# Fifteen block products for eighteen in layer 1, and its context in quarters of the array

## The chip, the cores and the metric

The kernel runs on one core of a Trainium2 chip. The metric is the device time of one execution in microseconds; the time before is the median of 3 runs. The engines are named as in the profile: PE multiplies matrices, PEld loads its weights, DVE, ACT and POOL work on vectors, and SP issues the DMAs. Products are in fp32 throughout.

## The reference

The program is two graph layers on 128 graphs of 64 nodes with 768 features. After each layer comes a residual and a layer norm. Cut to what is computed:

```python
def layer0(x, adj):                       # 12 heads of 64
    h = einsum('bnd,ade->bane', x, W)
    th = tanh(h)
    a = th @ w_src + swap(th @ w_dst)
    a = where(a >= 0, a, 0.2 * a)
    a = softmax(where(adj, a, -999.0))
    f = elu(concat_heads(a @ h + b))
    gate = sigmoid(x @ H_w.T + H_b)
    return gate * f + (1 - gate) * x

def layer1(x, adj):                       # 6 heads of 128
    q, k, v = heads(x @ Wq + bq), heads(x @ Wk + bk), heads(x @ Wv + bv)
    s = q @ k.T / sqrt(128) + where(adj, 0, -9e15)
    return concat_heads(softmax(s) @ v) @ Wf + bf

x = layernorm(x + layer0(x, adj))
x = layernorm(x + layer1(x, adj))
```

Layer 0 has two dense products of 768x768 (W and H_w), layer 1 four (Wq, Wk, Wv, Wf). The attention products are small: 64 nodes by 64 nodes for each head.

## The kernel before

**Tiles.** Two graphs fill the 128 partitions of a token tile, so there are 64 tiles, two tiles make a pair (32 pairs), and in phase B two pairs make a group (16 groups).

**Dense products.** Every 768x768 product of a pair is done by a 2x2x2 scheme: the two tiles are the rows, the two halves of the inner dimension and the two halves of the outputs (384) the other axes, and seven block products stand for eight. `Product` takes them one at a time (`matmuls(i)`, `evict(i)`), each as three matmuls of 128 rows (`CH` = 3). The sums of token blocks that the scheme needs are four additions on POOL (`token_sums`: S0 to S3, 384 columns each). The sums of weight blocks are made once for each weight (`weight_sums`: four additions of 1152 columns). Partial results leave PSUM by ACT copies ("snap") and DVE additions. PSUM tiles are called X (two buffers), Y and Z (one each), and pa or pb for the small products.

**Phase A** does layer 0, and layer 1's V product at its end, because its weights fit beside the others. It spills to DRAM: the normalized x (`x1_d`), its transposed form (`xT_d`), the four sums S (`S_d`) and v (`v_d`). Layer 0's aggregate (L476) multiplies 64x64 blocks: its row half and its column half pick a quarter of the array, 24 matmuls for a tile. The input is cut into chunks for the transposes (`chunk0`, L308) by features that lie 6 apart.

**Phase B** does the rest of layer 1. For a group it loads T (`T4`, one buffer) and S, then runs the Q and K products for three column blocks j of each half: weights stand still and 256 token columns (two pairs) move. `scores` then takes 8 matmuls for each head (L749), six batches a group. `sm_top` and `sm_total` do the softmax: maximum and subtraction on DVE, exp on ACT, sum and reciprocal on DVE, scaling on POOL (L771). `probs` transposes the probabilities (L776) and writes them by four ACT copies into `pt1`, a tile that holds a block diagonal of two graphs with zeros beside it, so that `context` can use whole 128x128 matmuls (L794), six for a tile. The output product F of a pair then adds into the residual tile x, to which POOL has added the bias before (`add_bf`, L674). `layernorm` takes its statistics on DVE and three small instructions on POOL (L221, L223, L224), `normalize` is one ACT instruction (L228), and SP stores the tile.

**Order.** Nothing is scheduled by a planner. Each phase is a table of events: `at(step, f)` puts a function into a step, and `run` calls the steps in order. The functions emit instructions on all engines, so the table fixes the order of each engine's queue; semaphores do the rest. Phase B has 35 steps a group before:

```python
for j in range(3):
    at(o + 7 * j, lambda d=d, j=j: start_qk(d, j))
    for i in range(7):
        at(o + 7 * j + i, lambda d=d, i=i: dense_qk(d, i))
    at(o + 7 * j + 7, lambda d=d, j=j: scores(d, j, 0))
    at(o + 7 * j + 8, lambda d=d, j=j: scores(d, j, 1))
```

The output products of a group begin 56 and 63 steps after its first step, which are steps 21 to 34 of the next group, beside that group's last scores and its softmax; the last group draws them forward. The weights Wq and Wk come in at the end of phase A (`load_early`), in the places of layer 0's weights, and POOL makes their sums 30 and 46 steps after the last pair's first step.

## Time and profile before

| | |
|---|---|
| median of 3 runs | 3132.32 us (3130.44 to 3134.71) |
| the profiled execution's own time | 3132.67 us |
| its span, first to last instruction | 3130.7 us |
| instructions in the profile | 42352 |
| first Q matmul of phase B | 1603.84 us |
| PE busy | 3039.9 us, 97% of the span |
| POOL busy | 1292.9 us: 938.67 before 1603.8 us, 354.28 after |
| DVE busy | 1557.3 us: 999.82 before 1603.8 us, 557.45 after |
| ACT busy | 962.9 us |
| DMA | 309.40 MB, mean 99 GB/s |

Times are in microseconds unless marked ns. A row of the groups has line, engine, operation, output and inputs by the program's names, shapes and count, then busy time, the mean ns of one, and the idle time of the engine before these with what ended it. A row of the timeline has its start, its length, the engine, the line and what is merged in it. A row of the waits has who waited for whom, the total, the number of times and the longest. Matmuls are pipelined and overlap in the records, so the mean ns of one is longer than the distance between two starts. The digits are tenths of busy time in 40 slices of 78 us.

### The profile page before, as it was taken

What the parts mean: (1) busy time and instruction counts of PE and PEld (TensorE: products, weight loads), DVE (VectorE), ACT (ScalarE), POOL (GpSimd) and SP (SyncE); (2) the same over time, 40 slices, a digit from 0 to 9 for tenths busy, and PEclk for the clock granted to TensorE, in tenths of its full rate; (3) what the DMA queues carried; (4) which work ended last, traced back from release to release, by engine and by line L of the source; (5) the groups of instructions that cost most, each with busy time, mean ns of one, the idle gap of its engine ahead of it and who ended that gap; (6) DMA issues with size and microseconds to landing.
All of it is one profiled execution on the core that took longest, in us unless ns stands there. A gap on an engine that the chain in (4) does not pass through costs nothing.

```text
span 3130.7 us, 42352 instructions
## 1 busy us (share of the span) xinstructions
PE 3039.9 (97%) x16164; PEld 2124.8 (68%) x16164; DVE 1557.3 (50%) x2717; ACT 962.9 (31%) x1901; POOL 1292.9 (41%) x1207
## 2 busy tenths in 40 slices
PE   7999999999999999999878999999999999999998
PEld 4566666666666666666557777887777887777885
DVE  4666666666666666666612333334333334333334
ACT  2344444444344444443312221222221222221122
POOL 4656556566566566565532122222122222122223
PEclk9999999999999999999889999999999999999999
DMA  4233233333233333333432222212222212222211
GB/s 152 87 112 123 89 115 117 99 115 117 94 115 117 100 115 106 106 120 99 147 139 82 87 76 92 91 62 102 87 75 94 91 61 102 87 73 95 91 62 61
DMA packets 186218, 309.40 MB, mean 99 GB/s; under 512 B 89504, under 2 KB 115104, under 8 KB 186016
## 3 DMA queue, kind: packets, MB, share of 16 engines
q1 hardware_dynamic: 186016, 306.69, 29.2%
q8 instruction: 128, 2.10, 0.3%
q14 instruction: 74, 0.61, 0.1%
HBM read 167.81 MB, written 126.22 MB: 94 GB/s over the span
## 4 chain that ended last, share of the span: by engine, by line
PE 89%; DVE 4%; DMA 1%; ACT 1%; POOL 1%; issue 0%; SPq 0%; POOLq 0%; DVEq 0%
PE X L147 45%; PE Y L147 24%; PE Z L147 9%; PE pb L794 3%; PE pa L308 3%; PE pb L749 2%; PE pa L476 2%; PE pa L458 1%; DVE st L216 1%; PE pb L776 1%; DVE snap L820 1%; DVE s L762 1%; DVE sm L768 0%; DVE mx L761 0%; ACT s L763 0%
## 5 line engine op out<-in xcount | busy, mean ns | idle before, releaser
L147 PE MATMUL X<-w,S 128*128 128x384 f32 x1728 | 614.2, 492 | 6.0 <-DVE v L356 3.7
L147 PEld LDWEIGHTS X<-w,S 128*128 128x128 f32 x1728 | 320.5, 191 | 241.8 <-DVE gt L337 19.9
L147 PE MATMUL X<-S,w 128*128 128x256 f32 x1728 | 396.5, 379 | 0.0
L147 PEld LDWEIGHTS X<-S,w 128*128 128x128 f32 x1728 | 326.0, 190 | 43.1
L221 POOL TENSOR_TENSOR rstd<-rstd,neg_half 128x1 f32<-128x1 f32 x128 | 70.5, 551 | 652.7 <-DVE rstd L220 652.7
L771 POOL TENSOR_TENSOR s<-s,rs 128x768 f32<-128x768 f32 x32 | 47.1, 1473 | 627.3 <-DVE rs L770 584.6
L228 ACT ACTIVATE x<-x,shift,rstd 128x768 f32<-128x768 f32 x128 | 131.3, 1026 | 295.8 <-POOL shift L224 295.8
L147 PE MATMUL X<-w,T 128*128 128x384 f32 x576 | 209.0, 500 | 8.5 <-ACT T L309 7.3
L147 PE MATMUL X<-w,Sc 128*128 128x384 f32 x576 | 204.7, 492 | 12.0 <-DVE snap L820 12.0
L147 PE MATMUL Z<-w,T 128*128 128x384 f32 x576 | 205.3, 493 | 0.0
L147 PE MATMUL Y<-w,S 128*128 128x384 f32 x576 | 204.8, 492 | 0.0
L147 PE MATMUL Y<-T,w 128*128 128x256 f32 x864 | 202.2, 379 | 0.0
L147 PE MATMUL Y<-w,T 128*128 128x384 f32 x576 | 201.5, 486 | 0.0
L690 ACT COPY snapq<-X 128x256 f32<-128x256 f32 x192 | 71.5, 372 | 363.4 <-PE X L147 363.1
L147 PEld LDWEIGHTS Y<-T,w 128*128 128x128 f32 x864 | 163.0, 190 | 21.5
L147 PEld LDWEIGHTS X<-w,Sc 128*128 128x128 f32 x576 | 105.7, 190 | 86.7 <-DVE snap L820 21.9
L147 PEld LDWEIGHTS Y<-w,T 128*128 128x128 f32 x576 | 109.4, 190 | 76.3
L720 DVE SCALAR_TENSOR_TENSOR q<-X,bq_c,snapq 128x256 f32<-128x256 f32 x48 | 23.2, 484 | 267.8 <-PE X L147 267.8
L147 PEld LDWEIGHTS X<-w,T 128*128 128x128 f32 x576 | 107.5, 196 | 70.8 <-ACT T L309 9.0
L447 POOL TENSOR_TENSOR s<-s,rs 128x768 f32<-128x768 f32 x64 | 94.8, 1481 | 146.6 <-DVE rs L446 146.6
L147 PE MATMUL X<-T,w 128*128 128x256 f32 x576 | 138.2, 390 | 13.6 <-DMA T<-xT_d 13.6
L147 PEld LDWEIGHTS Y<-w,S 128*128 128x128 f32 x576 | 105.4, 191 | 62.2
(132 smaller groups left out, 5431.1 us busy)
## 6 DMA issues: line engine op xcount, KB each, us to landing
x<-in_x_dram SPq DMA_DIRECT2D x64, 384.0 KB
s<-dst_d SPq DMA_DIRECT2D x128, 192.0 KB
x_d<-x SPq DMA_DIRECT2D x64, 384.0 KB
xT_d<-T SPq DMA_DIRECT2D x64, 384.0 KB
S_d<-S SPq DMA_DIRECT2D x32, 768.0 KB
v_d<-v SPq DMA_DIRECT2D x128, 192.0 KB
T<-xT_d SPq DMA_DIRECT2D x32, 768.0 KB
S<-S_d SPq DMA_DIRECT2D x32, 768.0 KB
```

The lines of the kernel that those rows point to most:

```text
L147: nc.tensor.matmul(o, self.lhsT(i, c), rhs, start=first and c == 0, stop=last and c == CH - 1, skip_group_check=True,)
L216: nc.vector.bn_stats(st[:, half, :], r[:, halves(half)])
L221: nc.gpsimd.tensor_tensor(rstd, rstd, neg_half, ALU.pow)
L228: nc.scalar.activation(r, r, AF.Identity, bias=shift, scale=rstd)
L308: nc.tensor.transpose(ps[:, c, :], chunk(src, k), ident)
L447: nc.gpsimd.tensor_tensor(self.s, self.s, self.rs[:, :, None].to_broadcast([P, A, S]), ALU.mult)
L458: nc.tensor.transpose(ps[:, jj, :], self.s[:, 2 * j : 2 * j + 2, :].rearrange("p h m -> p (h m)"), ident,)
L476: nc.tensor.matmul(self.pos[h2][own, j, :], self.pt[rws, j, own], rhs, start=True, stop=True,)
L690: nc.scalar.copy(t, ps)
L749: nc.tensor.matmul(pc[own, q, i, :], qT[:, i, q, own], kT[:, i, q, own], start=True, stop=True)
L771: nc.gpsimd.tensor_tensor(s, s, rs[:, :, None].to_broadcast([P, A, S]), ALU.mult)
L794: nc.tensor.matmul(pc[:, jj, :], v[:, hd * P : (hd + 1) * P], pt1[:, hd, :], start=True, stop=True)
```

## The change

Phase B's three dense products (Q, K and the output product) use a 2x3x3 scheme: two tiles, three blocks of 256 inner features, three blocks of 256 outputs, and fifteen block products where eighteen would be plain. The tables `SUMS`, `WEIGHT_SUMS` and `STEPS` hold the scheme. A block product is two matmuls of 128 rows and 256 columns. Four PSUM chains accumulate and are read between steps: each step names the chain, and the outputs to which the chain's present value is added or from which it is subtracted. For Q and K the first touch of an output is an ACT instruction and the others are DVE additions; for the output product all 16 are DVE additions into the residual tile.

The eleven token sums are now made on POOL in phase B, for each group (512 columns, `group_sum`) and for each pair of the output product (256 columns, `pair_sum`); in the first group DVE makes seven of them. S is no longer stored and loaded. The weights of phase B have fourteen sums of 512 columns each (`weight15_sum`) in place of four. `S{k}`, `Sc{k}`, `T4` and the two tiles of scores have one buffer each.

The context works on 64x64 blocks: v is loaded so that the two heads of a couple lie in the two halves of the partitions (four DMAs a tile), the probabilities are copied once and not laid out as a block diagonal, and 24 matmuls for a tile go to the quarters of the array. Q and K now go one after the other, in two passes j over 15 steps each, and scores come twice a group, three batches in a row. A group has 90 steps; the output products of a group take steps 60 to 89 of the next one. In phase A the PSUM tiles X, Y and Z share one pool of four, and `chunk0` takes features that lie 3 apart, with W read in the same order.

```diff
+STEPS = [   # sum or block, weight slot, chain, first, last, outputs touched
+    (6, 4, 2, True, False, (0, -1, 0, 0, 0, 0)),
+    (7, 13, 3, True, False, (0, 0, 1, 0, 0, 0)),
...
-    psX = ctx.enter_context(tc.tile_pool(name="psX", bufs=2, space=bass.MemoryType.PSUM))
-    psY = ctx.enter_context(tc.tile_pool(name="psY", bufs=1, space=bass.MemoryType.PSUM))
+    psX = ctx.enter_context(tc.tile_pool(name="psX", bufs=4, space=bass.MemoryType.PSUM))
...
-            return src.rearrange("p (q c) -> p c q", c=NC)[:, k, :]
+            return src.rearrange("p (h q c) -> p h c q", h=2, c=CH)[:, k // CH, k % CH, :]
...
-                nc.sync.dma_start(S_d[d["p"]], d["S"])
...
-        at(o + 30, lambda: weight_sums(early[0], nc.gpsimd))
-        at(o + 46, lambda: weight_sums(early[1], nc.gpsimd))
+        for k in range(len(WEIGHT_SUMS)):
+            at(o + 18 + k, lambda k=k: weight15_sum(early[0], k, nc.gpsimd))
+            at(o + 32 + k, lambda k=k: weight15_sum(early[1], k, nc.gpsimd))
...
+        def group_sum(d, k, eng):
+            r0, r1, op = SUMS[k]
+            t = k1.tile([P, 2, 2, P], F32, name=f"S{k}")
+            eng.tensor_tensor(t, group_part(d, r0), group_part(d, r1), op)
+            d["S"][k] = t
+        def pair_sum(d, q, k):
+            r0, r1, op = SUMS[k]
+            t = k1.tile([P, 2, P], F32, name=f"Sc{k}")
+            nc.gpsimd.tensor_tensor(t, pair_part(d, q, r0), pair_part(d, q, r1), op)
+            d["Sc", q, k] = t
...
+            def step(self, i):
+                r, slot, chain, start, stop, coefs = STEPS[i]
+                if start:
+                    self.acc[chain] = psX.tile(self.shape, F32, name="X")
+                ps = self.acc[chain]
+                for c in range(2):
+                    nc.tensor.matmul(ps, self.lhsT(r, slot, c), self.rhs(r, slot, c),
+                                     start=start and c == 0, stop=stop and c == 1,
+                                     skip_group_check=True)
+                for j, coef in enumerate(coefs):
+                    if coef and j not in self.begun:
+                        self.first(j, coef > 0, ps)
+                        self.begun.add(j)
+                    elif coef:
+                        self.add(j, coef > 0, ps)
...
-            for half in range(2):
-                pc = psa.tile([P, CH, P], F32, name="pb")
-                for jj in range(CH):
-                    hd = half * CH + jj
-                    nc.tensor.matmul(
-                        pc[:, jj, :], v[:, hd * P : (hd + 1) * P], pt1[:, hd, :], start=True, stop=True
-                    )
+            for j in range(CH):
+                for g in range(2):
+                    own = slice(g * S, (g + 1) * S)
+                    for half in range(2):
+                        for h2 in range(2):
+                            rws = slice(h2 * S, (h2 + 1) * S)
+                            cols = slice(half * S, (half + 1) * S)
+                            nc.tensor.matmul(pcs[h2][cols, j, own], v[rws, g, j, cols],
+                                             pt[rws, j, own], start=True, stop=True)
...
+        R = len(STEPS)
+        N = 6 * R
...
+                at(o - 29, lambda g=g: load_T(g))
+                at(o - 35, lambda g=g: load_adj(g))
+            for k in range(len(SUMS)):
+                eng = nc.vector if g == 0 and k % 3 else nc.gpsimd
+                at(o - 24 + 2 * k, lambda d=d, k=k, eng=eng: group_sum(d, k, eng))
...
+                at(e + 3 + 6 * q, lambda d=d, q=q: sm_top(d, q))
+                at(e + 6 + 6 * q, lambda d=d, q=q: sm_total(d, q))
+                pr = o + (4 * R + 14 + 12 * q if last else N + 4 + 16 * q)
+                f = o + ((6 if last else 10) + q) * R
...
+                        s = max(f - R + max(SUM_STEPS[: k + 1]) + 1, pr + 13)
+                    at(s, lambda d=d, q=q, k=k: pair_sum(d, q, k))
+                at(f - (3 if last else 12), lambda g=g, q=q: load_x(g, q))
+                at(f - (1 if last else 5), lambda d=d, q=q: add_bf(d, q))
...
+                    s = f + R + 1 + 3 * i
+                    at(s, lambda d=d, q=q, i=i: norm1(d, q, i))
+                    at(s + 2, lambda d=d, q=q, i=i: norm2(d, q, i))
```

In the last lines, o is the group's first step, e is o + 62, q the pair of the group and f the step at which a pair's output product begins.

## The prediction

> **What bounds the kernel now.** I read the busy shares first, then PE's waits, then PE's timeline for the pace of each kind of matmul.

> ```profile
> PE 3039.9 (97%) x16164; PEld 2124.8 (68%) x16164; DVE 1557.3 (50%) x2717; ACT 962.9 (31%) x1901; POOL 1292.9 (41%) x1207
> ...
> PE   7999999999999999999878999999999999999998
> ...
> POOL 4656556566566566565532122222122222122223
> ```

> PE shows 9 in 35 of 40 slices. POOL falls from 4 to 6 tenths in phase A (slices 1 to 20) to some 2 in phase B: that looks like room.

> ```profile
> PE X L147 <- DMA T<-xT_d: 13.6, 1, 13.6
> PE X L147 <- DVE snap L820: 12.0, 16, 1.7
> ```

> Of phase B, these and two waits of the first group (7.9 us, on POOL's softmax scaling and ACT's pt) are all that the view lists for PE. The first is the start of phase B, the second 0.75 us in each of 16 groups. Phase B runs from the first Q matmul (1603.84 us in the timeline) to the end; T loads of neighbouring groups stand 94.0 us apart (2019.58 and 2113.56). So phase B is priced by PE's passes. An fp32 matmul is two passes, two records.

> ```profile
> 2009.03 2.75 PE L147 MATMUL X<-S,w 128*128 128x256 f32 x12
> ...
> 2011.62 2.75 PE L147 MATMUL Y<-S,w 128*128 128x256 f32 x12
> ...
> 2024.00 0.69 PE L749 MATMUL pb<-k,q 128*64 128x64 f32 x16
> ...
> 2024.62 2.20 PE L147 MATMUL Z<-w,cT 128*128 128x384 f32 x6
> ...
> 2026.75 0.69 PE L749 MATMUL pb<-k,q 128*64 128x64 f32 x16
> ```

> Starts count, since matmuls overlap: 12 passes of 256 columns take 2.59 us, **216 ns each**. Six passes of 384 columns take 1.935 us (next fence), **322.5 ns each**. From one score batch to the next, 2.75 us, less those six passes, leaves **0.81 us** for a batch of 8 score matmuls. Single records inside the batch start 7 and 52 ns apart, so its matmuls take 8 x 59 = 0.47 us and the change of array mode 0.34.

> ```profile
> 1520.52 2.10 PE L147 MATMUL Z<-w,T 128*128 128x384 f32 x6
> 1522.45 2.10 PE L147 MATMUL X<-w,S 128*128 128x384 f32 x6
> ```
> ```profile
> 1503.43 2.10 PE L147 MATMUL X<-w,T 128*128 128x384 f32 x6
> ...
> 1506.32 2.20 PE L147 MATMUL Z<-w,T 128*128 128x384 f32 x6
> 1508.36 2.10 PE L147 MATMUL X<-w,S 128*128 128x384 f32 x6
> ```
> ```profile
> 2056.23 1.50 PE L794 MATMUL pb<-pt,v 128*128 128x128 f32 x12
> 2057.57 1.46 PE L147 MATMUL Z<-T,w 128*128 128x256 f32 x6
> ```

> In the middle stretch, layer 0's aggregate of one tile lies between the products: 24 matmuls of 64x64 in the array's quarters. 1508.36 - 1503.43 less two products (3.87) leaves **1.06 us a tile**, mode changes included. Layer 1's context with full matmuls takes 2 x 0.67 = **1.34 us a tile**: 12 passes, 1.34 us from the first start to the next line's start.

> [...] 48 quarter passes in 1.06 us, and 0.34 us of mode change around a score batch. [...] at 2045.46 POOL starts a norm only as the softmax scaling ahead of it ends, though DVE had its input ready at 2045.2. [...] The softmax subtraction, of one shape, takes 958 ns in phase B (L762) and 1374 in phase A (L437), where POOL is busy[...] Layer 0's transposes at a stride of 6 floats start 136 ns apart, unit-stride ones 109.5.

> **The change, PE's work, per group (16 of them).** Q and K: 2 x 3 x 21 matmuls become 2 x 2 x 30, of 256 columns: (240 - 252) x 0.216 = -2.6 us. Output product: 42 matmuls of 384 columns become 60 of 256: 120 x 0.216 - 84 x 0.3225 = 25.9 - 27.1 = -1.2. Context: 4 tiles x (1.06 - 1.34) = -1.1. Scores: 6 batches of 8 become 2 of 24: 2 x (24 x 0.059 + 0.34) = 3.5 against 4.9, -1.4. Transposes of the probabilities stay. Sum -6.2 us, **-99 us** in all. Phase A's chunks at a stride of 3 floats instead of 6: 12 transposes x 32 pairs x at most 27 ns = 0 to -10; I take -5. One shared pool of four PSUM tiles for X, Y and Z keeps a product's distance before a tile is reused: nothing. The S tiles' stores (768 KB a pair) and loads go, v comes in 16 DMAs a group for 4, at some 0.4 us each on SP: the DMA share is 1 to 3 tenths in phase B, SP issues a few times in 94 us, and after the start PE waits for no DMA, so nothing. pt's four copies become one on ACT, which is at 1 to 2 tenths: nothing.

> **What it adds: POOL.**

> ```profile
> L674 POOL TENSOR_TENSOR x<-x,bf_bc 128x768 f32<-128x768 f32 x64 | 114.0, 1813 | 6.3 <-DMA x<-x_d 6.3
> L771 POOL TENSOR_TENSOR s<-s,rs 128x768 f32<-128x768 f32 x30 | 44.2, 1473 | 580.7 <-DVE rs L770 541.1 <-DVE x L824 35.3 <-ACT pt L785 4.3
> L221 POOL TENSOR_TENSOR rstd<-rstd,neg_half 128x1 f32<-128x1 f32 x64 | 35.2, 550 | 249.5 <-DVE rstd L220 249.5
> L196 POOL TENSOR_TENSOR Sc<-cT 128x384 f32<-128x384 f32 x31 | 31.0, 999 | 253.7 <-DVE cT L799 253.5
> ```

> Sums of 384 columns take 1.00 us, of 768 1.81, of 1152 2.62: 0.18 + 2.13 ns a column. So a sum of 512 columns is estimated at 1.27 us and one of 256 at 0.73. Per group POOL gets 11 of the first (the next group's S) and 22 of the second (Sc), 30.0 us, for 8 sums of 1.00. Its total, 44 us of some 88, would fit. Its order does not. Take t = 0 at the group's step 60, when the output products begin. A step is 4 passes, 0.864 us; the 24 scores after step 62 add 1.76. Without waits the second pair's product begins at 14.7 (step 75), the next group at 27.7 (step 90). The program puts on POOL, in this order:
> - two Sc sums, then S0. T4 has one buffer, so its load goes out at 0, as the last Q and K pass has read it; on SP only loads stand ahead of it, into tiles long free. In the timeline 3.1 MB went from issue (2019.58) to the last byte in about 10 us; 1.6 MB needs half, with its start about 5.5. S0 ends at 6.8.
> - the first softmax scaling. The scores are done at 3.5. On DVE the maximum (0.94) and the subtraction (0.96) stand behind step 64's add and end at 8.7, exp (0.84) at 9.6, the sum and reciprocal (1.18) behind three more adds at 11.2. **POOL idles from 6.8 to 11.3**, with all that follows queued behind the scaling.
> - then without a gap: 2 scalings (2.9), S1 to S10 (12.7), 9 Sc (6.5), 2 additions of the bias (3.6), 4 norms of 0.55 + 0.19 + 0.19 (3.7), together 29.5. It ends at 40.8.

> Who waits: the two bias additions end at 22.0. The second product's first add on DVE needs them and could have begun at 15.7. A PSUM tile is written again three steps on, so an eviction has about 1.0 us to spare: PE stands some 5 us. Further on, the third norm's shift ends at 39.9. ACT's normalize (1.02) waits for it with the eviction of the new group's step 3 behind it (0.48). Step 6, in the same PSUM tile, starts at 41.5 in place of 32.9. **8.6 us a stretch**, the 5 included; [...] I take 9. Bounds: 5.5, if the scaling comes 2 us sooner and sums overlap a little; 12, if DVE's queue (below) adds. It happens in 14 stretches (the next S and the last pair's output product together): **+126 us**. The 12 us behind DVE's snap go, and waits of 1 us behind the contexts' two evictions (2 x 0.56 on DVE against 1.0 us to spare) take their place: zero.

> **End of phase A.** Eight weight sums of 2.62 us become 28 of 1.27, and 26 now stand ahead of the last pair's S sums, which the last V product needs; before, four did. 33 - 11 = 22 us more on POOL. It idled some 26 us there, in pieces between 1527 and 1577, which takes up part: 5 to 20, I take **+13**. Phase B's start: 0.8 MB less to wait for, one sum of 1.3 us and a bias load more: zero.

> **Sum.** -99 - 5 + 126 + 13 = +35 on the profiled execution's own 3132.7 us (span 3130.7), which is within 0.4 us of the median of the runs: **3167**.

> **Rivals.** (1) POOL keeps up: the low share and the sums' late deadlines (one or two steps before use) speak for it, FIFO order and the one-buffer T4 against. With the 1 us a group of now it gives -99 - 5 + 13 = -91, **3042**. The point that decides is a stall of (99 + 5 - 13) / 14 = 6.5 us a stretch; below it the change is faster. Chance 0.14. (2) DVE becomes the bound too. In the stretch it has 32 adds (0.43, scaled from 0.56 at 384 columns), 6 score evictions (0.29), 2 softmaxes (3.1) and two norms (1.45): 24.6 of 27.7 us. A softmax block of 1.9 us overruns the 1.0 to spare. Added on top, 12 us a stretch: **3209**, chance 0.2. It can't act alone, since its backlog also delays what POOL waits for. (3) The quarters don't run in parallel here: 48 passes at 52 ns, +1.5 us a tile, 96 us more, about **3260**; layer 0 shows the same shape in parallel, so 0.03. The forecast has 0.63.

> **Numbers.** Low: -99 + 14 x 5.5 + 5 - 10 = -27, 3105. High: -99 + 14 x 12 + 20 = +89, 3221. Within 0.2% (6 us, about what a measurement tells from no change) needs a stall between 6.1 and 7.0: 0.05. Faster takes rival 1 and a little of the forecast's low end, 0.15; slower 0.8.

> **What would show it.** PE's waits: X behind DVE and ACT at some 9 us a group, ended by POOL further back; T loads about 97 us apart; POOL at 6 to 9 tenths around the output products; Q passes still at 216 ns; a context at 1.06 us. If the T loads stand below 90 us apart, the POOL queue was read wrong; if the additions of the bias end before step 76, so was its order.

## The result and the profile after

The changed kernel takes **3187.32 us** (median of 4 runs, 3184.58 to 3189.33), the kernel before 3131.6 beside it: ratio **1.0176**, 95% interval 1.0158 to 1.0193. The spans of the two profiled executions are 3187.5 and 3130.7 us, 56.8 us apart. The forecast was 3167 in a range of 3105 to 3221, with 8 chances in 10 for slower: side and range held, and 22 us of the 57 were missing.

The page of the kernel after, its busy shares and slices:

```profile
PE 2990.1 (94%) x18852; PEld 2172.6 (68%) x18852; DVE 1783.0 (56%) x3364; ACT 935.3 (29%) x1709; POOL 1656.2 (52%) x1629
...
PE   6999999999999999999678999999999999999997
...
POOL 4556556556656656656733554334544335544345
```

PE has 50 us less work in the records and stands more. POOL has 363 us more; its slices in phase B, 3 to 5 tenths, still look like room. The waits of PE tell otherwise:

```profile
PE X L768 <- DVE x L809: 69.1, 27, 4.1
PE X L768 <- ACT q L789: 24.7, 14, 2.7
...
PE X L768 <- DMA w<-in_L_gnn_Wf_dram: 15.5, 1, 15.5
PE X L201 <- POOL S L251: 9.6, 1, 9.6
PE X L768 <- POOL S L738: 9.5, 3, 7.5
```

The first two are phase B's, in 14 stretches: an eviction on DVE (L809, an add of the output product into x) and one on ACT (L789, a first touch of q). Neither engine is the cause. Take the stretch whose step 60 starts at 2429.38 us. PE's timeline has both waits:

```profile
2446.18 1.03 PE L768 MATMUL X<-w,cT 128*128 128x256 f32 x4
2451.27 5.25 PE L768 MATMUL X<-w,Sc 128*128 128x256 f32 x12 [4.06 <-DVE x L809]
2456.35 1.03 PE L768 MATMUL X<-w,cT 128*128 128x256 f32 x4
...
2467.91 1.89 PE L768 MATMUL X<-S,w 128*128 128x256 f32 x8
2471.79 1.13 PE L768 MATMUL X<-T,w 128*128 128x256 f32 x4 [1.99 <-ACT q L789]
```

The releasers in turn waited for POOL, as the timelines of DVE and of ACT say in their brackets:

```profile
2450.80 0.42 DVE L809 TENSOR_TENSOR x<-x,X 128x256 f32<-128x256 f32 x1 [3.91 <-POOL x L726]
```
```profile
2470.35 1.03 ACT L281 ACTIVATE x<-x,shift,rstd 128x768 f32<-128x768 f32 x1 [3.83 <-POOL shift L277]
2471.28 0.45 ACT L789 ACTIVATE q<-X,bq_c 128x256 f32<-128x256 f32 x1
```

And POOL's own timeline shows how it came to be late:

```profile
2435.97 1.27 POOL L738 TENSOR_TENSOR S<-T 128x512 f32<-128x512 f32 x1 [3.89 <-DMA T<-xT_d]
2441.24 1.47 POOL L854 TENSOR_TENSOR s<-s,rs 128x768 f32<-128x768 f32 x1 [4.01 <-DVE rs L853]
...
2448.96 3.56 POOL L726 TENSOR_TENSOR x<-x,bf_bc 128x768 f32<-128x768 f32 x2
...
2470.13 0.19 POOL L277 TENSOR_TENSOR shift<-shift,neg_one 128x1 f32<-128x1 f32 x1
```

There are two idle spells of some 4 us, and behind the second the list runs without a gap for 30 us. The first addition of the bias ends at 2450.8, just as DVE's add starts. The third norm's shift ends at 2470.3, and ACT's normalize, with q's eviction behind it, starts there.

One thing in these lines no step of the prediction had. From 2451.27 to 2456.35 PE starts 12 passes in 5.08 us, where 12 took 2.59 in the kernel before: after its wait it runs at half clock (granted clock 0.50 from 2449.27 to 2456.09 us, 1.00 in the 4.27 us ahead of it and in the 3.41 behind). A row of the view by windows has the window, its length, the busy times of PE, PEld, DVE, ACT and POOL with their counts, and then the granted clock (0.96 and 1.00 here), the DMA share and GB/s. The first row goes from one T load (1846) to the load twelve groups on in the kernel after, the second over the same groups of experiment e3 below, where the long waits are gone:

```profile
1846.00:3010.10 1164.10, 1089.78 (x7921) 923.13 (x7920) 570.59 (x1404) 220.83 (x408) 518.73 (x612) 0.96 0.20 66
```
```profile
1846.00:2922.00 1076.00, 1056.13 (x7922) 896.08 (x7922) 572.77 (x1404) 221.77 (x408) 521.51 (x612) 1.00 0.23 72
```

The count of POOL's instructions (612) and its busy time are the same in both; the twelve groups take 97.0 us each in the one and 89.7 in the other.

### The profile page after: what moved, and what is told of

Read it like the earlier page. It is cut to its first block, busy times and chain, and to the rows that moved or that the text cites. A ratio compares the mean times of both kernels' runs of the same rounds, so it can differ in the third digit from the quotient of the medians.

```text
span 3187.5 us, 49046 instructions
## 1 busy us (share of the span) xinstructions
PE 2990.1 (94%) x18852; PEld 2172.6 (68%) x18852; DVE 1783.0 (56%) x3364; ACT 935.3 (29%) x1709; POOL 1656.2 (52%) x1629
## 4 chain that ended last, share of the span: by engine, by line
PE 63%; POOL 15%; DVE 12%; ACT 2%; DMA 2%; issue 2%; SPq 1%; DVEq 0%; POOLq 0%; ACTq 0%
PE X L201 28%; PE X L768 27%; POOL S L738 4%; POOL Sc L750 3%; PE pa L361 2%; DVE e L559 2%; PE pb L880 2%; POOL x L726 2%; POOL tmp L430 2%; PE pb L831 2%; POOL s L854 1%; POOL rstd L274 1%; DVE st L269 1%; SPq L713 1%; DVE e L560 1%
## 5 line engine op out<-in xcount | busy, mean ns | idle before, releaser
L201 PE MATMUL X<-w,S 128*128 128x384 f32 x2304 | 803.2, 492 | 17.7 <-POOL S L251 9.6
L768 PE MATMUL X<-S,w 128*128 128x256 f32 x2816 | 667.4, 385 | 25.5 <-DMA w<-in_L_gnn_Wf_dram 15.5
L201 PE MATMUL X<-w,T 128*128 128x384 f32 x1728 | 610.2, 493 | 10.3 <-ACT T L362 7.5
L768 PEld LDWEIGHTS X<-S,w 128*128 128x128 f32 x2816 | 532.0, 192 | 101.4 <-POOL S L738 27.1
L750 POOL TENSOR_TENSOR Sc<-cT 128x256 f32<-128x256 f32 x224 | 171.8, 776 | 669.1 <-PE X L768 490.2
L201 PEld LDWEIGHTS X<-w,T 128*128 128x128 f32 x1728 | 321.7, 192 | 210.8 <-issue 8.2
L768 PE MATMUL X<-w,Sc 128*128 128x256 f32 x1408 | 363.7, 411 | 70.7 <-DVE x L809 69.1
L768 PEld LDWEIGHTS X<-w,Sc 128*128 128x128 f32 x1408 | 281.4, 205 | 133.1 <-DVE x L809 77.4
L809 DVE TENSOR_TENSOR x<-x,X 128x256 f32<-128x256 f32 x512 | 203.4, 416 | 195.3 <-PE X L768 117.4
L794 DVE TENSOR_TENSOR k<-k,X 128x256 f32<-128x256 f32 x320 | 132.6, 421 | 264.1 <-PE X L768 235.4
L794 DVE TENSOR_TENSOR q<-q,X 128x256 f32<-128x256 f32 x320 | 133.6, 421 | 254.0 <-PE X L768 186.0
L768 PEld LDWEIGHTS X<-T,w 128*128 128x128 f32 x1024 | 192.7, 192 | 56.2 <-ACT q L789 30.3
L789 ACT ACTIVATE k<-X,bk_c 128x256 f32<-128x256 f32 x192 | 91.0, 474 | 353.4 <-PE X L768 353.4
L789 ACT ACTIVATE q<-X,bq_c 128x256 f32<-128x256 f32 x192 | 90.6, 473 | 311.9 <-PE X L768 294.5
L367 ACT COPY snap<-X 128x384 f32<-128x384 f32 x288 | 136.5, 479 | 93.8 <-PE X L201 89.8
```

What stands on the lines that cost most here:

```text
L201: nc.tensor.matmul(o, self.lhsT(i, c), rhs, start=first and c == 0, stop=last and c == CH - 1, skip_group_check=True,)
L367: nc.scalar.copy(t, ps)
L750: nc.gpsimd.tensor_tensor(t, pair_part(d, q, r0), pair_part(d, q, r1), op)
L768: nc.tensor.matmul(ps, self.lhsT(r, slot, c), self.rhs(r, slot, c), start=start and c == 0, stop=stop and c == 1, skip_group_check=True,)
L789: nc.scalar.activation(o[:, b], ps, AF.Identity, bias=bias[:, hd : hd + 1], scale=1.0 if positive else -1.0)
L794: nc.vector.tensor_tensor(o[:, b], o[:, b], ps, ALU.add if positive else ALU.subtract)
```

## The experiments

The theory (P): POOL's instructions stand in an order in which the bias and the norms queue behind a softmax scaling that comes late. The rivals: DVE has become a bound by its own load (D); the eleven sums are simply too much for POOL, or T's late load sets the end (T). Ratios are against the kernel before, run on the same chip; "T loads" is the mean distance of the T loads of neighbouring groups from group 2 to 15 (after: 96.9 us, before: 93.98).

### e1: the additions of the bias earlier

```diff
-                at(f - (3 if last else 12), lambda g=g, q=q: load_x(g, q))
-                at(f - (1 if last else 5), lambda d=d, q=q: add_bf(d, q))
+                at(f - (3 if last else 45), lambda g=g, q=q: load_x(g, q))
+                at(f - (1 if last else 38), lambda d=d, q=q: add_bf(d, q))
```

> The changed kernel, with x loaded and the bias added 38 steps before the output product in place of 5, so before the stretch with the output products (the last group as it was). Same work on every engine. Theory P (POOL's fixed order makes PE wait): PE's wait on DVE x (69 us in all) falls below 10, POOL's list of the stretch ends 3.6 us sooner, ACT's wait for the last shift stays; with the half-clock time that follows each long wait, 4 to 5 us a group less, 3115 to 3140 us. Rival D (DVE's 24.6 us of work in a stretch of 27.7 is what PE waits for): DVE has the same work in the same order, so within 10 us of the changed kernel, about 3180.

Measured: 3145.56 us (3134.25 to 3155.62), ratio 1.0051, interval 1.0031 to 1.0070; T loads 93.5 us. The median lies 6 us above what was expected. The executions spread over 21 us, and the granted clock with them: 0.983 in the profiled one, which is the shortest, and 0.975 in the longest. Waits of PE in e1:

```profile
PE X L768 <- ACT q L789: 52.4, 28, 2.8
...
PE X L768 <- DVE x L809: 6.2, 8, 1.9
```

The wait for DVE falls from 69.1 to 6.2 us with DVE's work untouched: it was a wait for POOL's bias. The other one doubles, as POOL's list still ends late and PE now comes to it without having stood before. So two places depend on one queue.

### e2: the softmax scaling later

```diff
-            nc.gpsimd.tensor_tensor(s, s, rs[:, :, None].to_broadcast([P, A, S]), ALU.mult)
+            d["rs", q] = rs
...
+                at(e + (6 + 6 * q if last else 25 + 11 * q), lambda d=d, q=q: sm_scale(d, q))
```

(sm_scale is that one POOL instruction in a function of its own.)

> The changed kernel, with the softmax scaling on POOL put 19 and 24 steps later into the program, behind the sums of the next group, so that nothing is queued behind its wait for exp (the last group as it was). Same work on every engine. Theory P: POOL's 4 us without work at 12 us of the stretch go, all that stands behind is 4 to 5.5 us sooner; PE's wait on DVE x falls to a quarter, that on ACT q by half; 3105 to 3135 us. Rival D: the same work on DVE at the same place, so about 3180. A third theory T (POOL waits for T4's load, not for the softmax): the load is unchanged, so most of the loss stays.

Measured: 3151.44 us (3150.46 to 3156.63), ratio 1.0062, 1.0047 to 1.0077; T loads 93.9 us. That is 16 us above what was expected. Waits of PE in e2:

```profile
PE pb L866 <- POOL s L858: 51.5, 15, 8.2
PE X L768 <- DVE x L809: 33.2, 47, 1.9
```

The wait for q on ACT is nearly gone (1.3 us in all). That for DVE halves, where a quarter was expected, and its longest falls from 4.1 to 1.9 us. A new wait takes their place, 8.2 us in the first group and 3.1 in each of 14 others: the transposes of the probabilities (L866) now wait for the moved scaling. With the bias still in POOL's list ahead of it, the place I had chosen was too late. A wait moved, not removed.

### e3: both moves

```diff
+                at(e + (6 + 6 * q if last else 25 + 11 * q), lambda d=d, q=q: sm_scale(d, q))
...
-                at(f - (1 if last else 5), lambda d=d, q=q: add_bf(d, q))
+                at(f - (1 if last else 38), lambda d=d, q=q: add_bf(d, q))
```

(x's load moves as in e1.)

> Both moves of order together. Theory P: POOL's list of the stretch ends some 8 us sooner, nearly when PE needs it; T loads 88 to 91 us apart, PE's waits on DVE x and ACT q below 20 us together, the granted clock back to 1.0 in steady groups; 3060 to 3100 us, faster than the kernel before. Rival D: 3170 to 3187, as the DVE work is untouched.

Measured: **3090.31 us** (3088.77 to 3091.11), ratio **0.9863**, 0.9849 to 0.9878: 97 us below the changed kernel and below the kernel before. T loads 89.7 us. Waits of PE in e3:

```profile
PE X L768 <- POOL S L738: 22.7, 2, 15.2
PE X L768 <- DVE x L809: 20.2, 29, 1.9
...
PE pb L866 <- POOL s L858: 8.1, 1, 8.1
```

The waits on DVE's x and ACT's q make 22.9 us together, a little above the 20 expected. Nothing is left out in e3: the 18852 matmuls, the 1629 POOL instructions (1660.1 us busy, after: 1656.2) and DVE's 3364 are those of the kernel after. Only the order differs. D and T fall with it: DVE's load and the sums are the same, and the first S sum still starts 6.6 us after step 60, as in the kernel after. The moves are worth 42 and 36 us alone and 97 together, since each alone leaves the other's wait or a new one, with some half clock behind it.

### e4: no sums of S after group 0

```diff
+            if d is not st[0]:
+                d["S"][k] = st[0]["S"][k]
+                return
```

Groups 1 to 15 use group 0's sums, so 14 us of POOL a group and all need of T on POOL are left out.

> The changed kernel without the sums of T for groups 1 to 15: they use group 0's sums, so Q and K of those groups are computed from other data, and 11 sums of 512 columns a group (14 us of POOL) are left out. Order of the rest as it was, so the softmax scaling still holds the additions of the bias behind it. Theory P: the wait on DVE x stays in part (2 to 3 us a group), the wait on ACT for the late shift goes; T loads 90 to 92 us apart, 3080 to 3110 us. Rival D: POOL's load doesn't matter, 3170 to 3187.

Measured: 3116.47 us (3114.11 to 3116.84), ratio 0.9946, 0.9931 to 0.9961. This is 6 us above what was expected; T loads 92.2 us. PE's wait for q on ACT is gone but for 1.8 us (POOL's list ends in time), and this is left:

```profile
PE X L771 <- DVE x L812: 45.6, 26, 3.2
```

Taking 14 us of a group away from POOL gains 71 us; keeping it and reordering gains 97. The bias still stands behind the scaling here, and half clock follows each of the 14 waits for it, 48 us in all, where e3 has none in the steady groups. This is order against load; but part of the 26 us between the two kernels is that half clock, so the 71 us are not what the load alone is worth.

### e5: the context in quarters, alone

The kernel before with the new loads of v, one copy of the probabilities, and the 24 matmuls of 64x64:

```diff
-            for half in range(2):
-                pc = psa.tile([P, CH, P], F32, name="pb")
-                for jj in range(CH):
...
+                            nc.tensor.matmul(pcs[h2][cols, j, own], v[rws, g, j, cols],
+                                             pt[rws, j, own], start=True, stop=True)
```

> The kernel before with layer 1's context alone in 64x64 blocks in the quarters of the array (v loaded in four DMAs a tile, one ACT copy of the probabilities); the dense products stay at seven block products, and the score batches stay six a group, so of the PE sum only the context's 4 x (1.06 - 1.34) = -1.1 us a group is taken over. Theory P: 16 x -1.1 = -18 us, a context 1.06 us of PE, no new wait: 3109 to 3121 us. Rival Q (the quarters don't run in parallel, or their mode changes cost more here): 3132 or above, up to 3230.

Measured: 3114.63 us (3113.12 to 3115.39), ratio 0.9945, 0.9930 to 0.9959; 17 us faster, T loads 92.8 us. The prediction's term was -1.1 us a group; it is -1.14. The sixteen DMAs of v for four bring no wait. Rival 3 is out.

### e6: the second weight's sums later at the end of phase A

```diff
-            at(o + 32 + k, lambda k=k: weight15_sum(early[1], k, nc.gpsimd))
+            at(o + 45 + k, lambda k=k: weight15_sum(early[1], k, nc.gpsimd))
```

> The changed kernel with the 14 sums of Wk put behind the last pair's S sums (13 steps later), so that only the 14 sums of Wq stand ahead of them. Theory P for the end of phase A: the last V product's wait for S (9.6 us) goes and the half-clock time after it, so the first Q matmul comes 8 to 14 us sooner, 1605 to 1611 us in the trace; the rest as in the changed kernel; 3173 to 3180 us. Rival: the last V product also waits for the chain before it (softmax, norm, transpose), so it gains under 4 us.

Measured: 3176.15 us (3170.48 to 3179.12), ratio 1.0139, 1.0124 to 1.0155; 11 us faster than the kernel after. The first Q matmul starts at 1605.13 us and not at 1618.87, and PE's 9.6 us behind POOL's S (L251) are gone: 14 of the 15 us by which phase A had grown are these sums, standing ahead of the last pair's S. The whole gains less than the 14, as phase B takes 3.6 us more in this trace than in that of the kernel after: PE waits for 104 us in both, but 7 us more are at half clock.

### e7: X, Y and Z in PSUM pools of their own again

```diff
+        PS["X"] = ctx.enter_context(tc.tile_pool(name="psX", bufs=2, space=bass.MemoryType.PSUM))
+        PS["Y"] = ctx.enter_context(tc.tile_pool(name="psY", bufs=1, space=bass.MemoryType.PSUM))
```

> The changed kernel with phase A's X (two buffers), Y and Z (one each) apart again, as in the kernel before; phase B keeps its four. The prediction held the shared pool at nothing. If that was right: no change, within 3 us. If the shared pool costs PE's 30 waits on ACT snap and some 1.8 us more in slower starts of a matmul in each phase A pair (5.9 us of waits in the view): phase A ends 6 to 10 us sooner, 3177 to 3182 us.

Measured: 3188.66 us (3185.01 to 3191.62), ratio 1.0181, 1.0166 to 1.0196: the same as after. PE's small waits for ACT's snap, 5.9 us in 30 pieces after and 0.4 in one before, stay (4.9 us, 28), so the shared pool did not make them.

### e9: the stride of phase A's chunks, alone

The kernel before with the features of a chunk 3 apart (and the weights read to match):

```diff
-            return src.rearrange("p (q c) -> p c q", c=NC)[:, k, :]
+            return src.rearrange("p (h q c) -> p h c q", h=2, c=CH)[:, k // CH, k % CH, :]
```

> The kernel before with only the chunks of layer 0 at a stride of 3 floats in place of 6 (W and H_w read to match). The prediction took -5 us, between 0 and -10, because the transposes start 23 ns sooner. If PE is the bound of phase A: 9 us faster, 3123 us, and phase A ends sooner. If what ACT has to copy is as near to the bound (the changed kernel shows 30 waits of X on ACT snap, 5.9 us, that the kernel before doesn't): transposes at some 113 ns, but X waits 5 to 6 us for ACT snap, and no change in all, 3128 to 3132 us.

Measured: 3130.79 us (3129.32 to 3134.33, 13 runs), ratio 0.9998, 0.9990 to 1.0006. The transposes themselves gain: the distances from each to PE's next start, before 1500 us, sum to 100.4 us and not 105.6. PE then waits, e9 first and the kernel before second:

```profile
PE X L147 <- ACT snap L314: 3.7, 21, 0.4
```
```profile
PE X L147 <- ACT snap L314: 0.4, 1, 0.4
```

All of PE's waits up to its first Q matmul grow by 4.1 us (60.8 to 64.9), against the 5.2 that the transposes give. So most of what they give, the products after them spend waiting, for ACT above all, and this is where most of the small waits looked for in e7 come from.

### e8: what the experiments point to

Both moves of e3 and e6, the PSUM pools of e7, two buffers for `Sc2`, and for the first groups: DVE shares group 1's sums, and group 0's scaling keeps its early place.

```diff
-            t = k1.tile([P, 2, P], F32, name=f"Sc{k}")
+            t = k1.tile([P, 2, P], F32, name=f"Sc{k}", bufs=2 if k == 2 else 1)
...
-                eng = nc.vector if g == 0 and k % 3 else nc.gpsimd
+                eng = nc.vector if g < 2 and k % 3 else nc.gpsimd
...
+                at(e + (6 + 6 * q if last or g == 0 else 25 + 11 * q), lambda d=d, q=q: sm_scale(d, q))
```

> The two moves of order together, with the late sums of Wk, phase A's PSUM tiles apart, a second buffer for Sc2, DVE sharing group 1's sums as it does group 0's, and the first group's scaling in its early place. Theory P: from 3090 us, 10 for the end of phase A, 0 to 7 for PSUM, 8 to 15 for group 1's begin: 3058 to 3076 us, with PE at 98% or more of phase B and T loads 89 to 90 us apart.

Measured: **3069.74 us** (3068.29 to 3071.32), ratio **0.9800**, 0.9784 to 0.9817: 62 us below the kernel before and 118 below the one after. T loads 89.8 us, first Q matmul at 1604.43, and the 8.1 us of e3 behind group 0's scaling are gone, with 4.5 us behind an addition of DVE to q in their place. The 7.3 us at group 1's start stay, though DVE helps with the sums: `T4` has one buffer, its load can go only when group 0 has read it, and group 0 has no output products before it to cover load and first sum. A second T4 wasn't tried.

## Why the prediction held, and where it missed

**The mechanism, moment by moment.** With t = 0 at step 60, predicted and measured in the stretch shown above: S0 ends at 6.8, 7.9; the scaling starts at 11.3, 11.9; the bias additions end at 22.0, 23.1; PE stands some 5 us, 4.06; the third norm's shift ends at 39.9, 40.9; step 6 of the new group starts at 41.5, 42.4. Sums of 512 and 256 columns, priced at 1.27 and 0.73 us, take 1.27 and 0.73. T loads: about 97, 96.9. That is the order of the queue as it was read.

**The stretch: 9 us, by another composition.** e3's 89.7 us a group, less its own listed waits of 1.7, leave 88.0 of work. In the same twelve groups the kernel after stands 73.3 us for DVE and ACT, 6.1 a group, and 97.0 - 88.0 - 6.1 = 2.9 is the rest: the slower passes. The granted clock is at half for 102 us in all between 1700 and 3050 us, in spells of 3.4 or 6.8 us, before never. The 9 came out right because the end of POOL's list sets the delay of step 6 (8.6 priced, to which I had added 0.4 as an estimate; 9.5 measured), into which the half clock falls as well as the two waits (4.06 + 1.99 in the stretch shown). In the three stretches where the spell at the first wait lasted 3.4 us and not 6.8, the second wait was 2.3 to 2.7 us; in the others it was 0.5 to 2.0. Shorter idle time came with it too: in e4 half clock follows each of 13 waits of 2.59 us. The prediction put no price on it.

**PE's work: -6.2 a group, -5.3 measured.** 93.98 less the 0.75 us of waits is 93.2 before; 88.0 after. The context's part is right (e5). The other 0.9 us are small delays: over the 216 and 322.5 ns of the pricing, the starts of the passes in e3 lose 1.7 us a group in pieces under 0.15 us, which the view of waits leaves out, and 0.8 before. What makes them stays open. The 0.9 does not show in the steady pace, because the 0.75 us behind DVE's snap went and nothing took their place, where I had set waits of the same size behind the context's evictions. Two errors, some 14 and 12 us in all, cancel: that is luck.

**The steps that failed** are mostly at the edges, and make up the 22 us:
- "Phase B's start: zero", and the same price a group for all 16. The 13 distances between T loads from group 2 to 15 add 38 us, predicted 36. Phase B outside them adds 3.3 us (305.1 before, 308.4 after), while three groups at -6.2 and one stretch at 9 made it -9.6. **13 us**. Some 3 of them are PE's work, -5.3 and not -6.2 in three groups. Some 7 lie at the end: the last group's output products are drawn forward, and DVE's additions wait three times for the bias there too (once POOL itself waits 2.9 us for the load of x). PE stands 7.8 us from 3060 us on, where the kernel before stood 3.2 from 2960 on, and has 7.8 us of half clock for 4.7. The begin of phase B gives only some 3: group 1 waits 7.5 us for T and the first sum and 2 more for later ones, but the kernel before stood 7.9 us there, behind group 0's softmax, with 10.2 us at half clock at that place in both. Waits of the last group (kernel after, from 3060 us) and of the first (before):

```profile
DVE x L809 <- POOL x L726: 7.3, 3, 3.5
```
```profile
PE pb L776 <- POOL s L771: 6.2, 1, 6.2
PE pb L794 <- ACT pt L785: 1.7, 1, 1.7
```

- "at most 27 ns ... I take -5" for the stride: **0**, not 5 (e9). The transposes do gain 5 us, but the next products then wait. A gain on PE was priced without asking what is late next.
- The end of phase A: +13, measured 15 with the stride's zero, 14 of it by e6. It is right but for 2 us, and the first Q product waits 2 us longer (15.5 against 13.6 before), which was priced at nothing.

5 + 2 + 13, and 2 in the steady groups, are the 22. The shared PSUM pool and the DMAs of v at nothing were right (e7, e5). The moves of e1, e2, e3 and e8 left the last group as it was. There the bias could go ahead as well; that wasn't tried.

**The rivals.** POOL keeps up (3042): false for this order, but e8 shows that nearly the same work in another order comes within 28 us of it. DVE as the bound (3209): false; e3 has all of its work in the stretch and keeps 20 us of short waits for it. The quarters not parallel: false (e5).

## What to carry to other kernels

A share of 3 to 5 tenths says nothing about a queue whose order the program fixes (the same 1629 instructions of POOL, two kinds of them moved, gave 97 us less): write down the order of its instructions with the time at which each input is ready, and look for one that is ready late ahead of others that are wanted soon. Put what is ready early and wanted soon ahead of it, and move both ends together, since either alone left a wait (42 and 36 us, against 97). Price the first and last groups apart, against what the kernel before loses there: their order and their cover are not those of the steady groups. And look at how long each wait of PE is, for one that brings half clock costs more than its length (after 4.06 us, another 2.49 over 12 passes).

## What the runs showed of the hardware

```profile
2257.83 1.43 PE L768 MATMUL X<-T,w 128*128 128x256 f32 x4 [2.76 <-ACT q L789]
...
2352.32 1.13 PE L768 MATMUL X<-T,w 128*128 128x256 f32 x4 [2.76 <-ACT q L789]
```
```profile
2258.00:2262.00 4.00, 4.00 (x55) 3.02 (x56) 1.67 (x4) 1.43 (x3) 0.10 (x1) 0.57 0.70 247
2352.50:2356.50 4.00, 4.00 (x63) 3.29 (x63) 1.83 (x5) 1.90 (x4) 0.73 (x1) 1.00 0.60 223
```

- POOL's fp32 sums with two inputs held the line of the prediction: 0.73 us at 256 columns and 1.27 at 512 (medians). Of the 352 sums of 256 columns in the kernel after, 15 took 1.44 to 1.46 us, and each of these began while DVE did the softmax subtraction (L845). No other took over 0.75, though 35 of them lay wholly in busy time of DVE.
- Transposes of fp32 read at a stride of 3 floats start 113 ns apart, against 134 at 6 (the prediction took 136) and 109 at 1, all medians.
